# Group statistics of the last image taken 18 steps into layer 3, and its first loads issued from ScalarE's queue into other buffers

## Chip, core and metric

The kernel runs on one core of one Trainium2 chip. The metric is the time on the device in microseconds (us), from the first to the last instruction of that core and what lies around them. The median of three runs of the kernel before is 3160.31 us (3152.64 to 3162.91).

A core has five engines with a queue of their own each: TensorE (PE; its weight loads are listed apart as PEld), VectorE (DVE), ScalarE (ACT), GpSimd (POOL) and SyncE (SP). Each works off its queue in order and waits for semaphores. SP computes nothing here: it issues DMA transfers. ScalarE can issue them too.

## The reference

Four residual layers on four images of 256 channels and 48 x 48 points, each after a group norm without weights:

```
x = x + L0(gn(x))     # attention over 49 dilated neighbours
x = x + L1(gn(x))     # 3x3 convolution of signs
x = x + L2(gn(x))     # 3x3 convolution, ternary weights, scale alpha
x = x + L3(gn(x))     # box-window linear attention, 8 heads

gn(v): m, s = mean and var over the 8 channels of a group and all points
       (v - m) / sqrt(s + 1e-5)

L3(x): q, k = sigmoid(Wq x), sigmoid(Wk x);  v = Wv x / |Wv x|
       for w in 1, 2, 4:                     # windows of 48, 24, 12 points
         attn = q . box_w(k v^T);  norm = q . box_w(k)
         out_w = attn / (norm + 1e-6)
       Wout [out_1, out_2, out_4] + bout
```

So layer 3 needs from each image two numbers for every channel, the mean and one over the deviation of its group, taken over the whole of layer 2's output.

## The kernel before

**Two parts.** The first part computes layers 0 to 2 image by image, with other work laid into its gaps, and stores each image's result to `x3_d` in HBM. The second part, from about 1413 us on, is layer 3 for all images. For image 0, queries, keys and values are projected in the first part already, beside layers 0 to 2 of the last image (`project_first`); for each other image they are projected inside layer 3, one image ahead of their use.

**Order.** `InOrder` wraps every engine, so that the instructions of an engine run in the order of the program text. Plain `nc.scalar` calls, as the loads of `wout_sb` and `bout_sb`, are not wrapped, but stand in ScalarE's text ahead of everything of layer 3. The first SP transfer after pools are opened may move ahead of SP transfers of the text before it; the queries' first load does (1405.23 us, before the last store of x).

**The statistics** (class `Stats`). `take` adds one block's moments on VectorE. `end` makes the group values: two aggregations; a tiny matmul with `gmat` that averages over a group; four VectorE operations; a second tiny matmul; one addition; then `rsqrt`, which takes a root on ScalarE and refines it by five VectorE operations. Between these it calls `wait`, which lays in filler work. `layer2` ends with `stats.end` and writes the image's factors to `st3`, which only the projections of that image read. For the last image that is deep in layer 3.

**Layer 2's end.** `give` adds a convolution's output, times `alpha`, to x on VectorE. After the last third of the rows it stores x (`x3_d`), 384 KB.

**Layer 3's loop.** Its unit is a block: image `b`, half of the heads `ct`, and eight rows `rb`. A block has some ten steps. In step `n` TensorE makes the scores of step `n` (`s`, out of queries `qs` and keys `ks`), VectorE, ScalarE and GpSimd mask them into `sm`, and TensorE sums step `n - 2` (`acc`, out of `sm` and values `vs`). `ps_s` has two buffers and a step uses both, so scores wait for the masks of the step before. At the fifth step of a block (`WHOLE`) the window states are added; they are made of the keys and values of the row blocks that are seen whole (`state`, `window_state`).

Beside this, `advance` is called once in a step and lets every waiting job (a Python generator: projections, running sums of keys `k_sums`, norms, states) go one piece further. A job says by `yield n` for how many steps it wants to rest. `bank` gives the one spare PSUM bank to one job in a step. `until` calls `advance` again and again until something is made; these forced steps count as steps. `FETCH` is 3, the rest after a load is issued.

**First loads.** Ahead of the loop come the first block's queries (`load_q`) and the keys and values of `seen_first` = 4 row blocks (`load_kv`), all on SP: 192 KB each. SP's later loads in the text are those of `k_sums` into `kp` (192 KB each) and of the projections into `xr` (384 KB each).

**Memory.** Pools are laid one behind the other in the order of the text, and layer 3's pools begin where those of the first part began. A tile of layer 3 waits for all uses of the earlier tiles whose place it takes. By the order and the sizes in bytes of a partition, counted from there: the first part has `wts` (0 to 1792, `alpha` last in it), then x in four buffers of 9216 (the last image in the third and fourth, up to 38656), then two operands of the convolutions of 25600 (the last image's in the second, 64256 to 89856), then weights. Layer 3 has `wts3` (0 to 15104, `wout_sb` with 6144 first in it), `kvp` (keys 15104 to 33536, values to 51968), then queries, and `sm` from 126464. So the first four keys lay on the x of the third image and, with a corner, of the last; the first values lay on the x of the last image and the first operand.

Of the kernel before, what the change touches and what calls it, by code (L numbers as in the profile page):

```python
# [12 lines left out]
F32 = mybir.dt.float32  # L13
# [9 lines left out]
P = 128  # L23
B, C, H, W = 4, 256, 48, 48
HW = H * W
NCT = C // P

RB = 8
NRB = H // RB
NB = RB * W  # L30
# [45 lines left out]
HEADS, D = 8, 32  # L76
WINDOWS = (1, 2, 4)
NW = len(WINDOWS)
HALVES = [H // w // 2 for w in WINDOWS]
# [4 lines left out]
LAG = 2  # L84
# [75 lines left out]


SEED = float(0x5F3759DF)


def penalties():
# [103 lines left out]
def conv_preact_kernel(  # L269
# [105 lines left out]
    def start(job, ahead=False):  # L375
        active.insert(0 if ahead else len(active), [step + 1, job])
# [60 lines left out]
    def paced(jobs, pace):  # L437

        for job in jobs:
            start(job)  # L440
            yield pace
# [172 lines left out]
    with (  # L614
# [50 lines left out]
        class Stats:  # L665
# [6 lines left out]
                dve.bn_stats(self.st[:, ct, s, :], xt[ct][:, s * RB : (s + 1) * RB, :])  # L672

            def end(self, wait):
                mv = small.tile([P, NCT, 2], F32, tag="gn_mv", name="gn_mv")
                for ct in range(NCT):
                    dve.bn_aggr(mv[:, ct, :], self.st[:, ct])
                m = small.tile([P, NCT], F32, tag="gn_m", name="gn_m")
                v = small.tile([P, NCT], F32, tag="gn_v", name="gn_v")
                r = small.tile([P, NCT], F32, tag="gn_r", name="gn_r")  # L680
                wait(1.5)
                ps = ps_st.tile([P, NCT], F32, tag="st", name="gn_ps")
                pe.matmul(ps, gmat, mv[:, :, 0], start=True, stop=True)
                dve.tensor_copy(m, ps)

                dve.tensor_sub(v, mv[:, :, 0], m)
                dve.tensor_mul(v, v, v)
                dve.tensor_add(v, v, mv[:, :, 1])
                wait(2.5)
                ps = ps_st.tile([P, NCT], F32, tag="st", name="gn_ps")  # L690
                pe.matmul(ps, gmat, v, start=True, stop=True)
                dve.tensor_scalar_add(v, ps, GN_EPS)
                rsqrt(r, v, NCT)
                return m, r
# [686 lines left out]
        def layer2(b, stats):  # L1381
# [100 lines left out]
                fetch_x(b + 2, 0)  # L1482
            fill(2)
            late()
            fill(1.5)
            m3, r3 = stats.end(fill)
            dve.scalar_tensor_tensor(st3[:, b, 0, :], m3, -1.0, r3, ALU.mult, ALU.mult)
            dve.tensor_copy(st3[:, b, 1, :], r3)

# [100 lines left out]
        with (  # L1590
            tc.tile_pool(name="xtp", bufs=3) as xtp,
            tc.tile_pool(name="bandp", bufs=1) as bandp,
            tc.tile_pool(name="smx", bufs=2) as smx,
        ):

            spread = smx.tile([QB, NPH * K0, HP], F32, tag="spread", name="spread", bufs=1)
            pool.memset(spread, 0.0)
            load_constants()
            prelude(1)
            batch_norm()  # L1600
            side = itertools.chain(prepare_layer1(), prepare_layer2())
            first = ExitStack()

            def project_first():

                scr, ps = (
                    first.enter_context(tc.tile_pool(name=name, bufs=2, side="right", **kwargs))
                    for name, kwargs in (("scr0", {}), ("ps_0", {"space": PSUM}))
                )
                for name, src in (("q", wq), ("k", wk), ("v", wv)):  # L1610
                    proj[name] = wts3.tile([P, NCT, C], F32, tag=f"w{name}", name=f"w{name}_sb")
                    sync.dma_start(out=proj[name], in_=src.rearrange("(ct p) o -> p ct o", p=P))
                groups = [(a, ("k0", "v", "q0")) for a in range(NRB)]
                groups += [(a, ("k1", "q1")) for a in range(NRB)]
                proj["first"] = Projection(0, scr, ps, "ps", [P, 512]), groups
                start(paced(proj["first"][0].groups(groups), 1))
                while active:
                    advance()
                    yield 1.2

            for b in range(B):
                if b + 1 < B:
                    filler = conv0(b + 1, {})
                else:
                    ending.close()
                    wts3 = ctx.enter_context(tc.tile_pool(name="wts_qkv", bufs=1, side="right"))
                    filler = project_first()
                    masks = wts3.tile([P, NMASK], BF16, name="masks")
                    nc.gpsimd.dma_start(out=masks, in_=masks_in[:, 0:NMASK])
                stats = attend(b)  # L1630
                for _ in side:
                    fill(1.5)
                load_wl1(0)
                load_wl1(1)
                load_wl2(0)
                layer2(b, layer1(b, stats))
                if b + 2 < B:
                    prelude(b + 2)
                else:
                    fill_all()  # L1640
            first.close()


    with (
        tc.tile_pool(name="wts3", bufs=1, reuse_waits="tile") as wts,
        tc.tile_pool(name="kvp", bufs=2 * NRB, reuse_waits="tile") as kvp,
        tc.tile_pool(name="qp", bufs=2, reuse_waits="tile") as qp,
        tc.tile_pool(name="scr", bufs=2, reuse_waits="tile") as scr,
        tc.tile_pool(name="smp", bufs=LAG + 1, reuse_waits="tile") as smp,
        tc.tile_pool(name="op", bufs=2, reuse_waits="tile") as op,  # L1650
        tc.tile_pool(name="ps_s", bufs=2, space=PSUM, reuse_waits="tile") as ps_s,
        tc.tile_pool(name="ps_acc", bufs=1, space=PSUM, reuse_waits="tile") as ps_acc,
# [202 lines left out]
        def load_kv(b, ct, a):  # L1855

            chans, cols = slice(ct * P, (ct + 1) * P), slice(a * NB, (a + 1) * NB)
            ks = kvp.tile([P, NKC, P], F32, tag="ks", name="ks")
            sync.dma_start(out=ks.rearrange("p k n -> p (k n)"), in_=k_d[b][chans, cols])
            vs = kvp.tile([P, NKC, HG, D], F32, tag="vs", name="vs")  # L1860
            sync.dma_start(
                out=vs, in_=v_d[b][:, a * NKC : (a + 1) * NKC, ct * HG : (ct + 1) * HG, :]
            )
            kvs[b, ct, a] = ks, vs
            if (b, ct) not in states:
                states[b, ct] = scr.tile([P, NRB, NKC, D], F32, tag="state", name="state")
            start(state(b, ct, a), ahead=True)

        def state(b, ct, a):

# [36 lines left out]
            wides[i] = t  # L1907
            made.add(("window", i))

        def load_q(b, ct, rb):  # L1910
            qs = qp.tile([P, W, RB], F32, tag="qs", name="qs")
            sync.dma_start(
                out=qs.rearrange("p w r -> p (w r)"),
                in_=q_d[b][ct * P : (ct + 1) * P, rb * NB : (rb + 1) * NB],
            )
            return qs
# [319 lines left out]
        def finish(i, stage):  # L2236
# [66 lines left out]
        seen_first = HALVES[0] // RB + 1  # L2303
# [27 lines left out]
        def midway(i):  # L2331

            b, ct, rb = order[i]
            if (b, ct) == (0, 0) and 0 < rb <= NRB - seen_first:
                a = seen_first - 1 + rb
                until(("k", 0, 0, a), ("v", 0, a))
                load_kv(0, 0, a)
            if ct == NCT - 1:
                start(prepare(i))
            if i + 1 < len(order):  # L2340
                start(window_state(i + 1), ahead=True)
                nb, nct, nrb = order[i + 1]
                until(("q", nb, nct, nrb))
                qs[i + 1] = load_q(*order[i + 1])

        def done(i):

            b, ct, rb = order[i]
            finishing.append((i, blocks.pop(i).stage))
            nb, nct = b + (ct + 1) // NCT, (ct + 1) % NCT  # L2350
            if nb < B:
                for a in LOADS.get(rb, ()):
                    until(("k", nb, nct, a), ("v", nb, a))
                    load_kv(nb, nct, a)


        stream = [
# [102 lines left out]
```

## Time and profile before

| | us |
|---|---|
| median of three runs | 3160.31 |
| the profiled execution | 3175.78 |
| its span, first to last instruction | 3174.0 |
| TensorE busy in the span | 2852.3 |
| TensorE's mean granted clock | 0.952 of full |
| last convolution's end to first scores | 1412.88 to 1416.64 |
| queries issued, first keys issued, first values issued | 1405.23, 1413.92, 1416.15 |
| `wout_sb` issued, first `kp`, first `xr` issued | 1416.87, 1424.68, 1425.73 |
| ScalarE's first mask of layer 3 | 1418.01 |
| TensorE busy in 1410 to 1430, 1430 to 1450, 1450 to 1470 | 12.62, 15.76, 20.00 of 20 each |

All times within the program are from the span's start, in the profiled execution. A line of the timeline gives the start, the length, the engine, the operation with the tile it writes and those it reads, and in brackets how long the engine had been idle before and what it waited for. `SPq` and `ACTq` are transfers being issued by SP and ScalarE; the length is that of the issuing, not of the transfer. The wrapper has one line of code for all engines, so operations are told apart by their tiles and not by lines.

### The profile page before, as it was taken

How to read it: one execution, taken by the hardware profiler on the slowest of the kernel's cores; microseconds unless marked ns; L12 is line 12 of the kernel's file. 1: busy time of each engine (PE TensorE's matmuls, PEld its weight loads, DVE VectorE, ACT ScalarE, POOL GpSimd, SP SyncE). 2: the span in 40 equal slices, each digit the busy share in tenths (PEclk: the TensorE clock that was granted, in tenths of full speed). 3: DMA queues.
4: the chain of work that ended last, by engine and by line, in shares of the span. 5: the costliest groups of instructions: out<-in, count | busy, mean ns of one | idle time of the engine just before them, and what ended most of it. 6: DMA issues, size and time to landing. Idle time of an engine off the chain costs nothing.

```text
span 3174.0 us, 99454 instructions
## 1 busy us (share of the span) xinstructions
PE 2852.3 (90%) x43082; PEld 2034.6 (64%) x43082; DVE 1989.3 (63%) x3779; ACT 991.4 (31%) x1959; POOL 1368.6 (43%) x1963
## 2 busy tenths in 40 slices
PE   3678999899989987889998899998999999999999
PEld 2556868677767866576665456665656666567665
DVE  7976658747864842276777565776546775555454
ACT  0002211121011134326643235552336533333322
POOL 0000012002000313046788876787856787744443
PEclk9889799999999998889999899999999999999999
DMA  8756412441333145324555665655644455611322
GB/s 277 214 161 188 154 68 103 127 127 49 132 114 113 57 124 158 113 80 138 160 181 174 184 203 157 183 174 161 169 127 145 142 173 156 166 41 43 97 73 66
DMA packets 380040, 434.10 MB, mean 137 GB/s; under 512 B 129843, under 2 KB 335443, under 8 KB 378451
## 3 DMA queue, kind: packets, MB, share of 16 engines
q1 hardware_dynamic: 378403, 425.76, 43.4%
q8 instruction: 341, 5.59, 0.7%
q0 software_dynamic: 144, 1.17, 0.2%
q10 hardware_dynamic: 1056, 0.79, 0.1%
q14 instruction: 96, 0.79, 0.1%
HBM read 288.11 MB, written 140.68 MB: 135 GB/s over the span
## 4 chain that ended last, share of the span: by engine, by line
PE 63%; DVE 11%; ACT 3%; POOL 3%; DMA 3%; issue 3%; SPq 1%; ACTq 0%; DVEq 0%; POOLq 0%
PE s L265 17%; PE cv L265 15%; PE acc L265 15%; PE out_ps L265 6%; PE proj_ps L265 5%; PE ap L265 3%; DVE sm L265 2%; DVE l2v L265 2%; ACT sm L265 1%; DVE v L265 1%; POOL sm L265 1%; PE keys_ps L265 1%; SPq L265 1%; DVE x L265 1%; DVE k L265 1%
## 5 line engine op out<-in xcount | busy, mean ns | idle before, releaser
L265 DVE TENSOR_TENSOR sm<-s,masks 128x448 f32<-128x448 f32 (+9 forms) x1408 | 620.1, 496 | 451.2 <-PE s L265 392.4
L265 POOL TENSOR_TENSOR sm<-sm,masks 128x704 f32<-128x704 f32 (+11 forms) x512 | 596.5, 1186 | 495.8 <-DVE sm L265 495.2
L265 ACT ACTIVATE sm<-s 128x384 f32<-128x384 f32 (+2 forms) x736 | 440.8, 608 | 734.2 <-PE s L265 583.9
L265 PE MATMUL cv<-vx,wt 128*128 128x288 f32 x2080 | 566.7, 429 | 90.5 <-DVE vx L265 49.2
L265 PE MATMUL s<-qs,ks 32*128 32x320 f32 (+10 forms) x8704 | 593.5, 361 | 36.7 <-ACT sm L265 26.3
L265 PE MATMUL acc<-sm,vs 128*32 128x128 f32 (+19 forms) x18432 | 606.6, 276 | 2.5 <-issue 2.1
L265 PEld LDWEIGHTS s<-qs,ks 32*128 32x128 f32 x8704 | 397.8, 186 | 264.1 <-issue 124.3
L265 PEld LDWEIGHTS acc<-sm,vs 128*32 128x32 f32 x18432 | 443.1, 110 | 176.5 <-issue 124.5
L265 PEld LDWEIGHTS cv<-vx,wt 128*128 128x128 f32 x2080 | 406.9, 200 | 213.6 <-issue 53.3
L265 POOL MEMSET v<- 128x16 f32 (+1 forms) x120 | 18.6, 214 | 765.2 <-DVE vx L265 639.0
L265 PE MATMUL cv<-v,wl 128*128 128x384 f32 x1152 | 227.2, 358 | 25.8 <-DVE x L265 8.2
L265 PEld LDWEIGHTS cv<-v,wl 128*128 128x128 f32 x1152 | 217.1, 198 | 37.0 <-issue 16.9
L265 DVE TENSOR_SCALAR sm<-s 128x896 f32<-128x896 f32 (+1 forms) x96 | 110.8, 1154 | 112.0 <-PE s L265 93.6
L265 PE MATMUL s<-masks 24*128 24x192 bf16 (+3 forms) x1664 | 169.2, 284 | 0.8 <-issue 0.8
L265 POOL TENSOR_TENSOR v<-l2v,v 128x384 fp32r<-128x384 f32 x96 | 108.4, 1158 | 119.5 <-ACT v L265 110.7
L265 PE MATMUL cv<-pad,wl 128*128 128x384 bf16 x864 | 145.6, 331 | 5.1 <-ACT pad L265 5.1
L265 POOL TENSOR_TENSOR nhi<-nhi,nq 128x384 f32<-128x384 f32 x144 | 147.3, 1044 | 0.0
L265 PE MATMUL out_ps<-o,wout_sb 128*32 128x384 f32 x1152 | 121.3, 490 | 7.2 <-ACT ns L265 3.7
L265 PEld LDWEIGHTS <-wl 128*128 128x128 bf16 x864 | 84.5, 98 | 65.6 <-issue 8.1
L265 PE MATMUL out_ps<-stage,wout_sb 128*32 128x384 f32 x1152 | 121.3, 487 | 0.0
L265 PE MATMUL ap<-seen,xT 120*128 120x120 f32 (+3 forms) x832 | 120.8, 306 | 0.0
L265 DVE TENSOR_TENSOR pt<-cs 128x184 f32<-128x184 f32 x144 | 120.4, 840 | 0.1
(176 smaller groups left out, 3398.6 us busy)
## 6 DMA issues: line engine op xcount, KB each, us to landing
wt<-wt SPq DMA_DIRECT2D x48, 768.0 KB
kb_d<-pt SPq DMA_DIRECT2D x48, 576.0 KB
rc<-r_d SPq DMA_DIRECT2D x192, 144.0 KB
nhi<-kb_d SPq DMA_DIRECT2D x120, 192.0 KB
nlo<-kb_d SPq DMA_DIRECT2D x88, 192.0 KB
o_d<-stage SPq DMA_DIRECT2D x24, 576.0 KB
o<-o_d SPq DMA_DIRECT2D x24, 576.0 KB
wl<-wl_d SPq DMA_DIRECT2D x16, 768.0 KB
```

Source lines behind the costliest of these rows:

```text
L265: return lambda *args, **kwargs: self.tc.keep_in_program_order(op(*args, **kwargs))
```

## The change

It has four pieces.

- `Stats.end` becomes a generator, `ending(room)`, that yields where it waited and takes its PSUM tile from `room`. `end` drives it, so that all other statistics stay as they were.
- For the last image `layer2` returns its `stats` with the aggregation not begun. A new job `moments`, started ahead of the loop of layer 3, rests for `6 * FETCH` = 18 steps, then runs `ending` with the spare bank `ps_m`, waits for its turn at the bank each time, and writes `st3` through `keep_moments`.
- The first queries, keys and values are issued by ScalarE (`queue=act`), after `wout_sb` and `bout_sb`; the four keys first, then the four values.
- The pools change order: queries and `sm` come right after `wts3`; `kvp` has buffers only for the row blocks below `SEEN_FIRST` = 4, and a new `kvp2` has those for the other two. By the same count, queries lie at 15104 to 18176, `sm` to 58880, the first keys at 58880 to 71168 and the first values from there to 83456.

```diff
+SEEN_FIRST = HALVES[0] // RB + 1
...
             def end(self, wait):
+                todo = self.ending(lambda: ps_st.tile([P, NCT], F32, tag="st", name="gn_ps"))
+                while True:
+                    try:
+                        wait(next(todo))
+                    except StopIteration as done:
+                        return done.value
+
+            def ending(self, room):
...
-                wait(1.5)
-                ps = ps_st.tile([P, NCT], F32, tag="st", name="gn_ps")
+                yield 1.5
+                ps = room()
...
-                wait(2.5)
-                ps = ps_st.tile([P, NCT], F32, tag="st", name="gn_ps")
+                yield 2.5
+                ps = room()
...
             late()
+            if b == B - 1:
+                return stats
             fill(1.5)
-            m3, r3 = stats.end(fill)
+            keep_moments(b, *stats.end(fill))
+
+        def keep_moments(b, m3, r3):
+
             dve.scalar_tensor_tensor(st3[:, b, 0, :], m3, -1.0, r3, ALU.mult, ALU.mult)
             dve.tensor_copy(st3[:, b, 1, :], r3)
...
-                layer2(b, layer1(b, stats))
+                last_stats = layer2(b, layer1(b, stats))
...
-        tc.tile_pool(name="kvp", bufs=2 * NRB, reuse_waits="tile") as kvp,
         tc.tile_pool(name="qp", bufs=2, reuse_waits="tile") as qp,
+        tc.tile_pool(name="smp", bufs=LAG + 1, reuse_waits="tile") as smp,
+        tc.tile_pool(name="kvp", bufs=2 * SEEN_FIRST, reuse_waits="tile") as kvp,
+        tc.tile_pool(name="kvp2", bufs=2 * (NRB - SEEN_FIRST), reuse_waits="tile") as kvp2,
         tc.tile_pool(name="scr", bufs=2, reuse_waits="tile") as scr,
-        tc.tile_pool(name="smp", bufs=LAG + 1, reuse_waits="tile") as smp,
...
+        def load_kvs(b, ct, rows, queue=sync):
+
+            new = {}
+            for a in rows:
+                chans, cols = slice(ct * P, (ct + 1) * P), slice(a * NB, (a + 1) * NB)
+                new[a] = (kvp if a < SEEN_FIRST else kvp2).tile([P, NKC, P], F32, tag="ks", name="ks")
+                queue.dma_start(out=new[a].rearrange("p k n -> p (k n)"), in_=k_d[b][chans, cols])
+            for a, ks in new.items():
+                vs = (kvp if a < SEEN_FIRST else kvp2).tile([P, NKC, HG, D], F32, tag="vs", name="vs")
+                queue.dma_start(
+                    out=vs, in_=v_d[b][:, a * NKC : (a + 1) * NKC, ct * HG : (ct + 1) * HG, :]
+                )
+                kvs[b, ct, a] = ks, vs
+                if (b, ct) not in states:
+                    states[b, ct] = scr.tile([P, NRB, NKC, D], F32, tag="state", name="state")
+                start(state(b, ct, a), ahead=True)
...
+        def moments():
+
+            yield 6 * FETCH
+            todo = last_stats.ending(lambda: ps_m.tile([P, 512], F32, tag="st", name="gn_ps")[:, 0:NCT])
+            while True:
+                try:
+                    next(todo)
+                except StopIteration as done:
+                    keep_moments(B - 1, *done.value)
+                    return
+                yield from bank(1, 0.0)
...
+        start(moments())
         for mo in range(NCT):
             start(k_sums(mo))
...
-        qs = {0: load_q(*order[0])}
-        for a in range(seen_first):
-            load_kv(0, 0, a)
+        qs = {0: load_q(*order[0], queue=act)}
+        load_kvs(0, 0, range(seen_first), queue=act)
```

More of the change, by code (lines that the diff above doesn't have):

```diff
@@ L1853, in inverse @@
             made.add(("norm", b, rb))
[L1855 to L1867, printed above, removed]
+        def load_kvs(b, ct, rows, queue=sync):
[13 more added lines that the diff above has]
+                start(state(b, ct, a), ahead=True)
         def state(b, ct, a):
@@ L1908, in window_state, with load_q @@
             made.add(("window", i))
-        def load_q(b, ct, rb):
+        def load_q(b, ct, rb, queue=sync):
             qs = qp.tile([P, W, RB], F32, tag="qs", name="qs")
-            sync.dma_start(
+            queue.dma_start(
                 out=qs.rearrange("p w r -> p (w r)"),
@@ L2301, in conv_preact_kernel @@
         start(in_turn(norms(b, rb) for b in range(B) for rb in range(NRB)))
-        seen_first = HALVES[0] // RB + 1
+        seen_first = SEEN_FIRST
         until(("q", 0, 0, 0), *((what, 0, *at) for a in range(seen_first) for what, at in (("k", (0, a)), ("v", (a,)))))
-        qs = {0: load_q(*order[0])}
-        for a in range(seen_first):
-            load_kv(0, 0, a)
+        qs = {0: load_q(*order[0], queue=act)}
+        load_kvs(0, 0, range(seen_first), queue=act)
         LOADS = {2: (0,), 3: (1, 2), 4: (3, 4), 5: (5,)}
@@ L2336, in midway @@
                 until(("k", 0, 0, a), ("v", 0, a))
-                load_kv(0, 0, a)
+                load_kvs(0, 0, (a,))
             if ct == NCT - 1:
@@ L2353, in done @@
                     until(("k", nb, nct, a), ("v", nb, a))
-                    load_kv(nb, nct, a)
+                    load_kvs(nb, nct, (a,))
         stream = [
```

## The prediction

> **What bounds the kernel now.** I read first the page's shares and its slices, to see which engine is full in which stage.
>
> ```profile
> span 3174.0 us, 99454 instructions
> PE 2852.3 (90%) x43082; PEld 2034.6 (64%) x43082; DVE 1989.3 (63%) x3779; ACT 991.4 (31%) x1959; POOL 1368.6 (43%) x1963
> ...
> PE   3678999899989987889998899998999999999999
> ...
> PEclk9889799999999998889999899999999999999999
> ```
>
> One slice is 79.4 us. TensorE is the bound nearly everywhere, so time that it stands idle at the edited place reaches the end. That place is the passage from layer 2 to layer 3, at 1413 us. I read next the chain of waits there (start, length, what), then the timeline (in brackets the idle time before an instruction and what ended it).
>
> ```profile
> 1395.14 17.74 PE cv L265 x96
> ...
> 1412.91 0.63 DVE x L265
> ...
> 1413.55 2.53 DMA x_d<-x
> ...
> 1417.57 7.26 DMA ks<-k_d
> 1424.83 0.14 issue
> 1424.97 2.51 PE s L265 x36
> ```
>
> ```profile
> 1415.02 0.30 PEld L265 LDWEIGHTS gn_ps<-gn_mv,gmat 128*128 128x128 f32 x2 [2.48 <-DVE gn_mv L265]
> ...
> 1416.24 0.30 PEld L265 LDWEIGHTS gn_ps<-gn_v,gmat 128*128 128x128 f32 x2 [0.92 <-DVE gn_v L265]
> ...
> 1416.64 1.15 PE L265 MATMUL s<-qs,ks 32*128 32x320 f32 x16
> ...
> 1416.86 0.20 ACT L265 ACTIVATE rsq_s<-gn_v 128x2 f32<-128x2 f32 x1 [18.22 <-DVE gn_v L265]
> 1416.87 0.43 ACTq L1656 DMA_DIRECT2D wout_sb<-in_wout_dram  x1
> ...
> 1419.26 1.58 SPq L265 DMA_DIRECT2D vs<-v_d  x1
> ```
>
> The reader is to see three things. The last convolution ends at 1412.88 and the first scores start at 1416.64: 3.76 us, in which TensorE does only the statistics. ScalarE's queue stands still for 18.22 us before `rsq_s`, and the load of `wout_sb` leaves 0.01 us after it. And the chain does not run through the statistics at all: it runs through the store of x and the third load of keys, which lands at 1424.83. The clock, in a table of one-microsecond windows (last three columns: granted clock, DMA share, GB/s), completes it:
>
> ```profile
> 1417.00:1418.00 1.00, 0.87 (x20) 0.48 (x12) 0.77 (x5) 0.06 (x1) 0.00 (x0) 1.00 0.53 157
> 1418.00:1419.00 1.00, 0.00 (x0) 0.00 (x0) 0.96 (x5) 0.49 (x1) 0.00 (x0) 0.52 1.02 282
> ...
> 1423.00:1424.00 1.00, 0.00 (x0) 0.00 (x0) 1.00 (x3) 0.55 (x2) 0.10 (x1) 0.50 1.09 359
> ...
> 1429.00:1430.00 1.00, 1.00 (x32) 0.86 (x28) 0.00 (x0) 0.08 (x1) 0.00 (x0) 1.00 0.73 216
> ```
>
> From 1418 to 1424.7 the DMA engines are full, and the clock is halved until about 1428.5.
>
> **What the Trainium skill says.** "DMA: Bandwidth & Descriptors", section "Queues, rings and completion order": each issuing queue has its own ring on each of the same 16 engines, a ring is consumed in its order, and an engine takes turns between rings packet by packet. The trace agrees: the keys issued at 1417.57, beside the output weights on the other ring, took 7.26 us, against 2.53 us for a store of twice the size. "TensorE: Matmul & The Clock Gate", section "Part 1: The HAM clock gate": after an idle window of about 3.4 us the clock is halved, and it comes back after about as long a busy one. Here 3.76 us of near idleness precede 0.50, and it returns some 3.5 us after work becomes dense at 1424.97. "ScalarE: Activation LUTs", section "What ACT_TABLE_LOAD costs": 1283 ns, and about 1380 ns of draining; the trace has 1283 ns for each of its 21, and doesn't show the draining.
>
> **Part 1, the statistics leave the passage.** Two pairs of tiny matmuls, two aggregations and some twelve VectorE operations of 0.15 to 0.3 us go. Taken alone this saves less than 3.76 us: the first keys were issued only at 1413.92, behind the store of x in SP's order, and the store and these keys (589 KB) were moving until 1416.2 (windows of 261, 270 and 58 GB/s). So the keys would have held the scores until about 1416.3 anyway; the saving without the load edit is about 0.3 us. It also frees ScalarE's queue from the wait for `rsq_s`.
>
> **Part 2, the loads move.** They are nine: one of queries, four of keys, four of values, 192 KB each. In ScalarE's order they stand behind `wout_sb` and `bout_sb`, which are written ahead of them. When can `wout_sb` leave? ScalarE's layer 2 work ends with a table load at 1398.64, so the queue is free. But by the sizes in the code `wout_sb` (6144 bytes in a partition) is the first tile of layer 3 and lies where the pool `wts` was, and that pool ends with `alpha`, which the last `give` reads until 1413.53. I take it that `wout_sb` waits for this read. Before, `rsq_s` hid that wait. So: `wout_sb` at 1413.57, 0.43 to issue; `bout_sb` 0.55; queries at about 1414.65, first keys 1415.1. The queries were issued at 1405.23 before, so this is later by 9.4 us, and the first keys by 1.2.
>
> What is worse, 768 KB of `wout_sb` are now ahead of queries and keys in the same ring. On SP nothing holds back the two `kp` loads (192 KB each, before at 1424.68, behind the last values) and `xr` (384 KB, before at 1425.73): I expect them right behind the store, at 1413.9 to 1415. Until the first keys land these must move: store 393 KB, `kp` 393, `xr` 393, `wout_sb` 786, queries 197, keys 197, together 2359 KB. The windows from 1417.5 to 1424.8 moved about 2160 KB in 7.2 us, so 0.30 MB in a microsecond: 7.9 us from 1414.2, so 1422. If the ring of `wout_sb` gets more than half I get 1421; if `kp` and `xr` come later, 1571 KB, so 1419.5. I take 1421.5: the first scores 4.9 us later than before.
>
> From there the pace is set by the masks, two score buffers being all there are: second scores about 4.2 us later (half clock), third again 4.2, so 1429.9 against 1424.97, also +4.9. Before, the third waited about 1.0 us for its keys (ScalarE was done at 1423.95), and now their keys are there in time; but the first scores now run at half clock (2.2 us for 1.15), which takes it back. The new places of the tiles are otherwise harmless: `sm` now overlaps the last image, whose store lands at 1416.08, before the first mask; the fourth keys and the values overlap layer 2's last operand, free at 1412.88. What follows until 1446, when TensorE waits for the windows' states, is a chain of the same steps and shifts as a whole. Sum of parts 1 and 2: +4.9, between +1.5 and +7.
>
> **Part 3, the statistics inside layer 3.** Eighteen steps counted with the forced ones come out near 1475 to 1490. In 1470 to 1490 TensorE is busy 19.53 of 20, VectorE 15.91, ScalarE 12.06. First half: two aggregations (0.25 each), four operations of 0.16, with gaps 1.2 us on VectorE, beside TensorE's accumulation. Second half: one operation, then a table load of 1.28 and the root of 0.20 on ScalarE, for which VectorE waits, then seven operations (1.3). Behind VectorE's wait stand the next step's masks, and behind those the scores. About 2.9 us against some 0.8 us of slack in a step of 3.4 leaves up to 2. Then the sigmoids' table comes back (1.28); before, one such load stood at 1445.63, where ScalarE was idle for 4.45 us after it, and the root's at 1397.36 in idle time too. The trace before shows no such switch in the steady part: at least 0 (all of it beside slack), at most 4 (both loads with the page's draining, an estimate). I take +2. The two uses of the bank push projections of image 1 back by two steps, far from due: 0.
>
> The split pools keep as many buffers per row block as before, and keys before values is without effect later, where single blocks are loaded: 0.
>
> **Sum.** +4.9 + 2 = +7 in the profiled execution: its own time was 3175.78 (span 3174.0), so about 3183. The median of the runs, 3160.31, lies 15.5 lower; carried over to it: 3167. That is +0.2%. A measurement of this kernel can tell about 0.3% (9.5 us) from no change.
>
> **Rivals.**
> *A, the loads leave early.* If `wout_sb` need not wait for `alpha`, all loads go out from 1398.6 and are there at 1412.88. Scores start 3.7 us earlier, the third ones 1.0 more, and the gap is too short for the half clock, worth about 3 (6.7 us of matmuls in 1418 to 1428 at half rate); less 2 of part 3: -6, 3154; at best -10. For it: the 18 us of idle ScalarE queue. Against: the overlap of addresses.
>
> *B, slower: ScalarE is held by issuing.* Eleven issues now stand ahead of its first mask. With full rings an issue took SP 1.58 us (values at 1419.26, queries at 1426.63), and a load of `kp`, due next, left SP only at 1424.68, so completions can hold issues back. Nine at 1.58 from 1414.65 end at 1428.9 instead of the 1423.8 when scores want a mask: +5 on top, +12, so 3172. It decides from a mean issue of 1.0 us. For it: full DMA; against: a mean issue of 0.45 for the rest, and keys need few descriptors.
>
> *C, a ripple.* From 1730 to 1775 TensorE is busy only 25.6 of 45 and GpSimd 39.25: image 0's norms are late there. Two shifted steps could move that by 8 us, either way: with +7, 3175 or 3159.
>
> **Chances.** Forecast 0.42 (0.34 within 0.3%, 0.08 slower), A 0.20 (0.12 faster, 0.08 within), B 0.28 (0.22 slower, 0.06 within), C 0.10 (0.06 slower, 0.03 faster, 0.01 within). Together: faster 0.15, within 0.49, slower 0.36. The range from 3150 to 3181 takes in A's middle, B, and the unknown costs of parts 2 and 3.
>
> **What would show it.** Right: `wout_sb` issued at 1413.6, scores at about 1421, no `gn_ps` before them, two table loads near 1480. Wrong: queries issued before 1413 (A); ScalarE still issuing values while finished scores wait (B); or scores before 1417 with `wout_sb` ahead of them, which would mean the rings share otherwise than I assumed.

## The result, and the profile after

The changed kernel takes 3205.60 us in the median of five runs (3194.39 to 3209.57); the kernel before took 3160.31 beside it. The ratio is 1.0131, with a 95% interval from 1.0111 to 1.0151: 1.3% slower, 45 us. The forecast was 3167, with a range up to 3181.

The page of the changed kernel, its shares and then its slices (here 80.1 us each):

```profile
span 3203.2 us, 99462 instructions
...
PE 2852.2 (89%) x43082; PEld 2031.6 (63%) x43082; DVE 2000.6 (62%) x3779; ACT 994.1 (31%) x1968; POOL 1369.6 (43%) x1963
...
PE   3678999898989977879997999898999999999999
...
PEclk9789799999999987889998999899999999999999
```

TensorE is as long busy as before (2852.3 us there). The loss is time in which it stands. Three slices from the passage on are one tenth lower than the same slices were before, and one, the 23rd, is one tenth higher. The lower ones are the 18th (1361 to 1441, the passage), the 22nd (1682 to 1762) and the 26th (2002 to 2082).

**What to compare.** The first part of the program is the same in both kernels, but it ended at 1402.8 in this profiled execution and at 1412.9 in that of before; over the sixteen kernels profiled here it ended between 1395.2 and 1412.9. So I compare times from the end of the last convolution. From there to the last instruction it is 1761.1 us before and 1800.4 after: +39.3. Kernels whose medians equal that of before lie between -4.8 and +4.0 by this measure, so a single such number is good to about 5 us.

The score products (8704 matmuls `s<-qs,ks`) come in the same order in every kernel, so the start of the n-th of them, from the last convolution's end, tells where a kernel falls behind. Differences to the kernel before, in us, worked out from the traces; image 0 ends at 2176, the first half of image 1 at 3264:

| n-th score product | 0 | 200 | 350 | 1400 | 1850 | 2300 | 3200 | 4400 | end |
|---|---|---|---|---|---|---|---|---|---|
| changed kernel | 4.7 | 6.0 | 7.9 | 4.6 | 11.0 | 9.5 | 35.2 | 44.3 | 39.3 |
| e1, two turns only | 0.0 | 0.4 | -0.9 | -4.4 | 2.5 | 1.3 | 28.2 | 34.3 | 30.5 |
| e12, one turn | 4.7 | 6.8 | 10.2 | 10.5 | 11.9 | 12.4 | 11.3 | 12.6 | 10.1 |
| e11, passage mended | -3.1 | -0.2 | -0.2 | 0.4 | 5.4 | 4.7 | 6.6 | 10.2 | 6.4 |

The passage costs about 6 us, near what was foreseen. The rest arises far behind the change, most of it in the first half of image 1. Between the 1400th and the 1850th product the changed kernel is up to 54 us behind for a while and has nearly caught up at the 1700th (13.6): the same steps of work come there in another order, as is shown below.

**The passage.** The chain of waits of the changed kernel there:

```profile
1385.07 17.72 PE cv L266 x96
...
1402.81 0.63 DVE x L266
...
1404.34 7.97 DMA kp<-kf_d
...
1412.33 0.33 ACTq L266
...
1412.70 0.45 ACTq L266
...
1414.87 0.88 ACT sm L266 x2
...
1415.80 2.86 PE s L266 x16
```

Its timeline (start, length, engine, operation, idle time before it and what ended that):

```profile
1403.46 0.44 ACTq L1671 DMA_DIRECT2D wout_sb<-in_wout_dram  x1
1403.87 1.16 SPq L266 DMA_DIRECT2D kp<-kf_d  x2
...
1405.23 7.43 ACTq L266 DMA_DIRECT2D ks<-k_d  x4
...
1411.21 2.09 PE L266 MATMUL s<-qs,ks 32*128 32x320 f32 x16 [8.44 <-DMA ks<-k_d]
```

`wout_sb` leaves 0.69 us after the last convolution, right after the last `give`; first scores come 8.44 us after it, 3.76 before. ScalarE issues keys and values until its first mask at 1414.87, 1.4 us after VectorE's first (1413.48): it is held, but little. By the chain one of its issues, that of the fourth keys at 1412.33, was held until `kp`, which SP had issued, had landed (1404.34 and 7.97 later).

**Where the larger part sits.** The same 160 us, counted from the start of the span, in the stretch table (busy time and number of instructions for PE, PEld, DVE, ACT, POOL, then granted clock, DMA share, GB/s). Before:

```profile
1950.00:2110.00 160.00, 154.27 (x3557) 101.89 (x3552) 114.79 (x207) 91.15 (x192) 127.32 (x193) 0.98 0.52 160
```

and after, followed by the waits of TensorE in 1930 to 2110 (what waited, for what, us in total, times, longest):

```profile
1950.00:2110.00 160.00, 140.22 (x3038) 90.97 (x3034) 102.91 (x181) 80.23 (x168) 117.06 (x156) 0.91 0.50 155
```

```profile
PE proj_ps L266 <- ACT sg L266: 18.0, 3, 7.7
PE s L266 <- ACT sm L266: 1.5, 1, 1.5
```

Before, the longest of these waits was another, and short:

```profile
PE proj_ps L265 <- ACT sq L265: 4.2, 1, 4.2
```

Every engine does less, the clock falls from 0.98 to 0.91, and TensorE makes 3038 matmuls in place of 3557. It stands three times for some 6 us because a projection's sigmoid (`sg`) is not done. ScalarE's own line at one of these places, and SP's queue ahead of it:

```profile
1955.34 0.49 ACT L266 ACTIVATE sg<-proj_ps 128x384 f32<-128x384 f32 x1 [8.28 <-DMA q_d<-sg]
```

```profile
1940.79 0.34 SPq L266 DMA_DIRECT2D nr<-n_d  x1
1941.23 0.38 SPq L266 DMA_DIRECT2D nq<-qr_d  x1
...
1949.26 1.53 SPq L266 DMA_DIRECT2D nlo<-kb_d  x1
1950.89 0.38 SPq L266 DMA_DIRECT2D qr_d<-kt  x1
1951.31 0.43 SPq L266 DMA_DIRECT2D q_d<-sg  x1
```

The sigmoid wants one of two `sg` buffers, whose store (`q_d<-sg`) stands in SP's order behind 16 loads for a block's norms (1941.2 to 1950.8; the expectations of e7, e9 and e13 give 30 and 14). Nothing of this touches the statistics or the first loads. An earlier trace of it is in the output products, `out_ps`, of the first finished block (block 6). Before:

```profile
1673.29 0.83 PE L265 MATMUL out_ps<-o,wout_sb 128*32 128x384 f32 x8
```

After:

```profile
1704.92 1.51 PE L266 MATMUL out_ps<-o,wout_sb 128*32 128x384 f32 x8 [2.38 <-ACT ns L266]
```

It comes 31.6 us later (41.7 from the last convolution), and its result is stored at 1750.86 in place of 1693.21. That gave the theory.

**The theory, "order".** Running the program's own order of jobs step by step shows that the spare bank is given away or held in every step from 70 to 137. The statistics take steps 85 and 88. All projections of image 1 behind them move on: the last value product of row block 4 goes from step 124 to 130, that of row block 5 from 139 to 141.

The bank is not what then delays block 6: it stands free from step 142 to 149, and block 6's output product does not ask for it. It waits for its preparation (`prepare`), three multiplications by one over the norms on GpSimd (`o<-o,rc`). GpSimd's time is shared out among the jobs like the bank, by `pool_turn`, and the jobs are asked in the order of a list, in which that of row block 4's values stands ahead of the preparation. After its last value product a row block scales its values on GpSimd. Before, row block 4 did this in steps 126 to 136, and block 6's preparation got all three of its turns in step 137. Now the scaling fills steps 136 to 138; the preparation gets one turn in step 139, and running sums and norms take the next ones. The other two come in step 150, where the loop forces steps because it needs block 6 done. GpSimd's trace shows the three multiplications together before:

```profile
1658.14 2.92 POOL L265 TENSOR_TENSOR o<-o,rc 128x384 f32<-128x384 f32 x3
```

and after one alone, the other two 45 us later, with a product of TensorE waiting for them:

```profile
1666.74 1.01 POOL L266 TENSOR_TENSOR o<-o,rc 128x384 f32<-128x384 f32 x1
...
1711.63 1.95 POOL L266 TENSOR_TENSOR o<-o,rc 128x384 f32<-128x384 f32 x2
1712.68 1.51 PE L266 MATMUL out_ps<-o,wout_sb 128*32 128x384 f32 x8 [4.97 <-POOL o L266]
```

So block 6's output product moves from step 141 to 153. The loop has to force nine steps for block 6 at its position 78, where it forced eleven for block 7 at position 89. From there on norms, stores and projections fall on other steps than in the kernel before, and the total stays at about the same number of steps (570 before, 569 now). The rival is that the moved work costs by itself: the statistics' instructions, the late loads, the new buffers.

### The profile page after: what moved, and what is told of

It is laid out like the page before. It is cut to its first block, busy times and chain, and to the rows that moved or that the text cites. A ratio compares the mean times of both kernels' runs of the same rounds, so it can differ in the third digit from the quotient of the medians.

```text
span 3203.2 us, 99462 instructions
## 1 busy us (share of the span) xinstructions
PE 2852.2 (89%) x43082; PEld 2031.6 (63%) x43082; DVE 2000.6 (62%) x3779; ACT 994.1 (31%) x1968; POOL 1369.6 (43%) x1963
## 4 chain that ended last, share of the span: by engine, by line
PE 61%; DVE 13%; POOL 4%; ACT 3%; DMA 3%; issue 2%; SPq 1%; ACTq 0%; DVEq 0%; POOLq 0%
PE s L266 17%; PE cv L266 15%; PE acc L266 14%; PE out_ps L266 5%; PE proj_ps L266 5%; DVE sm L266 3%; PE ap L266 3%; DVE l2v L266 2%; POOL sm L266 2%; SPq L266 1%; ACT sm L266 1%; DVE v L266 1%; POOL nhi L266 1%; PE keys_ps L266 1%; DVE x L266 1%
## 5 line engine op out<-in xcount | busy, mean ns | idle before, releaser
L266 PE MATMUL s<-qs,ks 32*128 32x320 f32 (+10 forms) x8704 | 602.4, 363 | 48.2 <-ACT sm L266 29.5
```

The source lines that it names most:

```text
L266: return lambda *args, **kwargs: self.tc.keep_in_program_order(op(*args, **kwargs))
```

## The experiments

Medians are of the runs of each kernel; ratios are against the kernel before on the same chip (its medians: 3165.04 for e1 to e4, 3163.74 for e5 to e8, 3163.40 for e9 to e11, 3168.35 for e12 to e14). The last column is the difference from the last convolution to the end, in one profile.

| kernel | median us | ratio, 95% interval | layer 3, us |
|---|---|---|---|
| changed kernel | 3205.60 | 1.0131 [1.0111, 1.0151] | +39.3 |
| e1 two turns only | 3194.54 | 1.0093 [1.0074, 1.0111] | +30.5 |
| e2 statistics late | 3180.48 | 1.0057 [1.0040, 1.0074] | +9.5 |
| e3 loads on SP | 3197.44 | 1.0103 [1.0084, 1.0121] | +37.6 |
| e4 late, weights last | 3177.87 | 1.0043 [1.0027, 1.0058] | +8.7 |
| e5 one turn only | 3163.52 | 0.9997 [0.9986, 1.0009] | -1.5 |
| e6 six turns only | 3172.20 | 1.0023 [1.0012, 1.0035] | +8.4 |
| e7 changed, one store on ScalarE | 3205.79 | 1.0131 [1.0108, 1.0153] | +35.2 |
| e8 before, the same | 3165.06 | 1.0000 [0.9984, 1.0017] | -4.8 |
| e9 changed, stores a step earlier | 3209.01 | 1.0147 [1.0112, 1.0182] | +39.3 |
| e10 before, the same | 3174.00 | 1.0027 [1.0014, 1.0040] | +10.3 |
| e11 passage mended, statistics hidden | 3170.99 | 1.0022 [1.0009, 1.0034] | +6.4 |
| e12 changed, one turn | 3177.85 | 1.0026 [1.0014, 1.0039] | +10.1 |
| e13 changed, norm loads split | 3203.56 | 1.0116 [1.0096, 1.0136] | +37.5 |
| e14 before, the same | 3169.32 | 1.0001 [0.9984, 1.0018] | +4.0 |

**e1: the two turns alone, in the kernel before.** The job issues no instruction; only the order of the others changes. By the program it is exactly that of the changed kernel, step by step.

```diff
+        def two_turns():
+
+            yield 6 * FETCH
+            yield from bank(1, 0.0)
+            yield from bank(1, 0.0)
...
+        start(two_turns())
         for mo in range(NCT):
             start(k_sums(mo))
```

> The kernel before, with one job added that does nothing but claim the spare bank for one step twice, from the 18th step on (it gets steps 85 and 88); statistics, loads and pools stay as before. Theory 'order' (two turns taken from the fully booked bank re-order the projections, norms and stores of images 0 and 1, and that is what costs): most of the +45 us, so +33 to +42 us over the kernel before, 3193 to 3202 us, with the same gaps of TensorE between 1950 and 2225 us. Rival 'instructions' (the loss is in the moved statistics' own instructions and in the later first loads): nothing is issued here, so within 5 us of the kernel before.

Measured: +29.5 us in the median, +30.5 in layer 3, a little less than "order" gave. Its stretch and its waits, for the same window as above:

```profile
1950.00:2110.00 160.00, 139.65 (x3002) 90.26 (x3006) 102.67 (x181) 81.19 (x169) 118.51 (x159) 0.92 0.51 157
```

```profile
PE proj_ps L265 <- ACT sg L265: 18.6, 3, 7.8
```

They are nearly those of the changed kernel, without one instruction of statistics and with all loads where they were. The rival falls for the larger part of the loss.

**e2: the statistics where the bank is free.**

```diff
         def moments():
 
-            yield 6 * FETCH
+            yield 27 * FETCH
```

> The changed kernel with the statistics 81 steps into layer 3 in place of 18, where the bank is booked by nobody (steps 148 and 149): all side jobs then run in the steps of the kernel before. Theory 'order': only the passage (+5.0 us in the profile) and up to 4 us of the statistics are left, so +3 to +9 us over the kernel before, 3163 to 3169 us. Rival 'instructions', or any loss by the new pools and queues: it stays near the changed kernel, +35 us or more.

Measured: +9.5 in layer 3 and +15.4 in the median, so some 30 us of the loss are gone; by the median it is 6 us more than the upper end of what I expected. It loses 6.0 in the passage and 4.6 at the statistics, of which about 1.5 come back.

**e3: the loads back on SP**, in the new buffers.

```diff
-        qs = {0: load_q(*order[0], queue=act)}
-        load_kvs(0, 0, range(seen_first), queue=act)
+        qs = {0: load_q(*order[0])}
+        load_kvs(0, 0, range(seen_first))
```

> The changed kernel with its first queries, keys and values issued by SP again, in the new buffers; the statistics stay 18 steps into layer 3. Theory 'order': only the passage gets its 5 us back, last convolution to first scores 3.4 to 4 us, so 3 to 8 us below the changed kernel, +36 to +42 us over the kernel before. Rival 'queue' (the loads through ScalarE delay everything that follows): back to within 10 us of the kernel before.

Measured: +32.4 in the median and +37.6 in layer 3, which is only 1.7 below the changed kernel. Layer 3 alone is within what was expected, and not by the stated path: the first scores were still 8.1 us after the last convolution, not 3.4 to 4. ScalarE issued `wout_sb` at 1407.42, before SP's first keys at 1408.26, and these were then waited for. So the queue of the loads hardly matters (1.5 us at the 200th product). That 768 KB of weights leave ahead of the keys is what is left; e4 tests it.

**e4: weights behind queries, keys and values, with the statistics late.**

```diff
-        nc.scalar.dma_start(out=wout_sb, in_=wout.rearrange("(kt p) o -> p kt o", p=P))
-        nc.scalar.dma_start(out=bout_sb, in_=bout.rearrange("(ct p) -> p ct", p=P))
...
         load_kvs(0, 0, range(seen_first), queue=act)
+        act.dma_start(out=wout_sb, in_=wout.rearrange("(kt p) o -> p kt o", p=P))
+        act.dma_start(out=bout_sb, in_=bout.rearrange("(ct p) -> p ct", p=P))
```

> The changed kernel with the statistics 81 steps in, as in e2, and the output weights and their bias issued by ScalarE after the first queries, keys and values instead of ahead of them. Theory 'order' with my account of the passage: queries and the first keys no longer wait behind 768 KB, first scores at most 3.5 us after the last convolution, so -5 to +1 us against the kernel before, and 4 to 9 us below e2. Rival (ScalarE is held by the issuing itself, not by the weights): as e2, within 2 us.

Measured: +12.8 in the median, 2.6 below e2: a miss, and the rival was nearer. The timeline of e4:

```profile
1405.72 1.15 PE L266 MATMUL s<-qs,ks 32*128 32x320 f32 x16 [0.71 <-DVE x L266]
...
1409.40 2.44 ACTq L266 DMA_DIRECT2D vs<-v_d  x4
...
1412.43 1.91 ACTq L266 DMA_DIRECT2D bout_sb<-in_bout_dram  x1
1414.44 0.87 ACT L266 ACTIVATE sm<-s 128x384 f32<-128x384 f32 x2 [24.96 <-DMA qs<-q_d]
```

First scores now start 0.71 us after the last convolution. But their mask waits behind ScalarE's issues until 1414.44, and TensorE waits 8.42 us for it. Of the 7.7 us won at the first scores 2.6 are left at the 200th product. This is the prediction's rival B, at a place where it decides.

**e5 and e6: one turn, six turns**, again in the kernel before. The edit of e1 for one turn; for six there are four such lines more than in e1.

```diff
             yield 6 * FETCH
-            yield from bank(1, 0.0)
             yield from bank(1, 0.0)
```

> As e1, but the added job takes one turn at the bank (step 85) and no second. Theory 'order' in its sharp form (the loss comes when the last value projections of image 1 are pushed onto step 141, where block 6's output product takes the bank before): with one turn less that product keeps its step, and norms and forced steps fall as in the kernel before, so within 5 us of it. Rival (every turn taken from a full bank costs alike): half of e1, +12 to +17 us.

> As e1, but with six turns at the bank (steps 85 and 88 to 92). By the order of the jobs six lost steps put norms and forced steps back to those of the kernel before. Theory 'order' in its sharp form: within 6 us of the kernel before, although three times as many turns are lost as in e1. Rival (turns cost alike): three times e1, +60 us or more; and if projections simply get too late, at least e1's +30.

Measured: one turn -0.2 us (0.9997), six turns +8.5 (1.0023; the expectation had 6). So the cost is not so much for a turn: none for one, 30 for two, 8 for six. What matters is who is pushed in front of whom. By the program's order, one turn leaves block 6's preparation its turns on GpSimd in steps 137 to 139, and the output product comes in step 142. Six turns push the values of row block 4 so far back that they come after the preparation, which has its turns in step 137 as before, and the product keeps step 141. In both, the forced steps stay where they were. In the trace of e6 the first output product starts at 1664.92 (259.0 from the last convolution; 260.4 before, 302.2 after). The sharp form in e5's expectation had the right result for another reason: it took step 141 of the bank for the place of the loss, but with two turns the bank is free in the eight steps after it.

**e12: the changed kernel with one turn.** All instructions, loads and buffers of the change stay; both products of the statistics are made in step 85.

```diff
+            yield from bank(1, 0.0)
             while True:
                 try:
                     next(todo)
                 except StopIteration as done:
                     keep_moments(B - 1, *done.value)
                     return
-                yield from bank(1, 0.0)
```

> The changed kernel with a single edit: the job of the statistics claims the bank once, at step 85, and makes both of its products in that one turn, in place of steps 85 and 88. Same instructions, same loads, same place. Theory 'order': one turn leaves norms and forced steps as in the kernel before (e5), so only passage (6 us) and the statistics' own time (2 to 5 us) are left: +8 to +14 us over the kernel before, some 30 us below the changed kernel. Rival (the second product so close behind the first stalls TensorE, or the loss hangs on what else the change does): +25 us or more.

Measured: +9.5 in the median, +10.1 in layer 3, so about 30 us below the changed kernel. Its stretch and TensorE's waits, as above:

```profile
1950.00:2110.00 160.00, 153.74 (x3606) 102.71 (x3606) 114.00 (x206) 91.79 (x192) 126.09 (x192) 0.99 0.52 159
```

```profile
PE proj_ps L266 <- ACT sq L266: 4.3, 1, 4.3
```

The waits for `sg` are gone and the clock is back. GpSimd's three multiplications for block 6 start at 1662.27, 1668.30 and 1672.26, within 11 us. With e1 this settles the cause: the second turn at the bank, and nothing that the change issues, makes 30 of the 39 us.

**e7, e9, e13: why the new order is worse.** Three edits of the changed kernel try to take away the waits for `sg`, each with a control in the kernel before (e8, e10, e14). None moves a job to another step. e7 and e8:

```diff
-            sync.dma_start(out=second[b][chans, cols], in_=t)
+            (act if b > 0 else sync).dma_start(out=second[b][chans, cols], in_=t)
```

> The changed kernel, with one of the two stores of a projection (the one that frees the sigmoid's buffer) issued by ScalarE in place of SP, for images 1 to 3. Theory: in the first half of image 1 sigmoids wait 26.3 us for stores that stand in SP's order behind the 30 loads of a block's norms, and TensorE's next projection waits 18.0 us for them; with the store on another queue this goes: 12 to 20 us below the changed kernel, still +20 to +33 us over the kernel before. Rival (TensorE's wait is replaced by GpSimd's lateness at the norms, or the issuing slows ScalarE's masks): within 6 us of the changed kernel.

> The same edit in the kernel before, as a control: there sigmoids wait only 1.9 us for such stores, so no gain is to be had by it; -4 to +6 us, the upper end if the issuing on ScalarE delays masks.

e9 and e10:

```diff
-            yield 1
             first, second = (qr_d, q_d) if name == "q" else (k_d, kf_d)
+            if b == 0:
+                yield 1
             sync.dma_start(out=first[b][chans, cols], in_=kt)
             sync.dma_start(out=second[b][chans, cols], in_=t)
+            if b > 0:
+                yield 1
```

> The changed kernel, with both stores of a projection (images 1 to 3) issued in the step of its sigmoid, ahead of the next step's jobs; all jobs keep their steps. Theory 'store behind the burst': the buffers of sigmoid and copy come free before the norms' 30 loads are issued, TensorE's 18.0 us of waiting for sigmoids in image 1 mostly go, 10 to 18 us below the changed kernel. Rival (the same turns of the bank are late wherever the stores stand, and norms' own loads wait instead, so GpSimd and TensorE are late there): within 5 us of the changed kernel.

> The same edit in the kernel before, as a control: little waiting for stores to take away (1.9 us for sigmoids, 6.6 us for values), so -5 to +4 us.

e13 and e14:

```diff
-            loaded = [load(ct) for ct in range(NCT)]
-            yield FETCH
+            loaded = [load(0)]
+            yield 2
+            loaded.append(load(1))
+            yield FETCH - 2
```

> The changed kernel with the loads of a block's norms issued in two halves two steps apart (the wait for them is shortened by as much, so every job keeps its steps). In image 1 the 14 loads in a row hold SP for 9.6 us (1941.2 to 1950.8) while two projections' stores stand behind them. Theory 'burst': TensorE's 18.0 us of waiting for sigmoids go down to 10 or less and 8 to 15 us are won against the changed kernel. Rival (TensorE's loss in image 1 isn't held by the burst alone, or the norms get their second half too late): within 5 us of the changed kernel, or above it.

> The same edit in the kernel before, as a control: nothing waits there for stores behind the norms' loads for more than 1.9 us; -3 to +6 us, the upper end if the second half comes late for GpSimd.

Measured: 1.0131, 1.0147 and 1.0116 against 1.0131 of the changed kernel: no gain, none, and at most 5 us. Each time TensorE's waits for `sg` shrink (9.8, 13.7 and 12.1 us in place of 18.0 in layer 3), and other waits grow. In e7 one sees how; ScalarE's part of the timeline:

```profile
1946.32 0.33 ACTq L266 DMA_DIRECT2D q_d<-sg  x1
...
1953.76 0.33 ACTq L266 DMA_DIRECT2D kf_d<-sg  x1
1954.19 0.49 ACT L266 ACTIVATE sg<-proj_ps 128x384 f32<-128x384 f32 x1 [4.60 <-DMA nhi<-kb_d]
1958.49 0.51 ACT L266 COPY kt<-sg 128x384 f32<-128x384 f32 x1 [3.81 <-DMA qr_d<-kt]
```

The store is issued early (1946.32; its sister `qr_d<-kt`, left on SP, at 1954.11), but ScalarE's next issue is held until 1953.76, by the trace until a load of the norms has landed, and then the copy `kt` waits for the other store, still behind the norms on SP. Among the controls e10 costs 10.6 us (1.0027) although it changes no job's step. That was not foreseen; I did not trace it. So that projections meet the norms' loads is what the traces show at these places, but no edit has shown that it holds the 25 us of image 1. More buffers for `sg` were not tried: one takes 1.5 KB of a partition, and 0.25 KB are free. That the second turn costs these 25 us is shown; through which wait it does so stays open.

**e11: all that was learned, put together.** Statistics in steps 160 and 161, where TensorE waits anyway; ScalarE issues queries and keys alone; values and then weights on SP (ScalarE's loads of the weights go, as in e4).

```diff
-            yield 6 * FETCH
+            yield 31 * FETCH
...
-                queue.dma_start(
+                sync.dma_start(
                     out=vs,
...
         load_kvs(0, 0, range(seen_first), queue=act)
+        sync.dma_start(out=wout_sb, in_=wout.rearrange("(kt p) o -> p kt o", p=P))
+        sync.dma_start(out=bout_sb, in_=bout.rearrange("(ct p) -> p ct", p=P))
```

> The changed kernel with three places mended: statistics 93 steps into layer 3, in steps 160 and 161, where TensorE waits 7.77 us for GpSimd's norms anyway; values on SP; output weights and bias on SP after them, so that ScalarE issues only queries and keys. Theory: the order is the one of before, first scores some 0.7 us after the last convolution as in e4 and masks no longer behind issues, statistics hidden: -4 to 0 us against the kernel before. Rival (statistics cost 3 us wherever they stand in layer 3, values are late behind the store of x): +2 to +6 us.

Measured: +7.6 us (1.0022), so the rival was nearer. The passage is no worse than before (first scores 3.1 us earlier, but only 0.2 are left of it at the 200th product). The statistics cost 5 us at their place, and another 4 are lost in the second half of image 1. The timeline of VectorE and GpSimd in e11 shows why the place was not free:

```profile
1721.44 0.16 DVE L266 COPY gn_m<-gn_ps 128x2 f32<-128x2 f32 x1 [0.48 <-PE gn_ps L266]
1721.60 2.52 POOL L266 TENSOR_TENSOR sm<-sm,masks 128x448 f32<-128x448 f32 x2
1721.63 1.04 DVE L266 TENSOR_TENSOR gn_v<-gn_mv,gn_m 128x2 f32<-128x2 f32 x1
1722.71 1.44 DVE L266 TENSOR_TENSOR gn_v<-gn_v 128x2 f32<-128x2 f32 x1
...
1730.59 0.92 DVE L266 TENSOR_SCALAR rsq_u<-rsq_u 128x2 f32<-128x2 f32 x1
```

Eight operations on two columns, 0.16 us nearly everywhere in e12, take 0.75 to 1.44 here, beside GpSimd's masks, norms and sums. The chain from 1720.48 to 1733.48, waits included, takes 13 us; in e12, at step 85, it took 4.3 (1474.67 to 1478.94). No version tried beats the kernel before.

## Why the prediction was wrong

- **Part 1, the statistics leave: not tested alone.** "About 0.3" was to be saved without the load edit, and no run moves the statistics and leaves all loads. e11 is 0.2 ahead at the 200th product, but its loads are other ones too.
- **Part 2, the loads: right in kind, in size with luck.** +4.9 was forecast, +4.7 measured at the first scores and +6.0 at the 200th. `wout_sb` left after `alpha`'s last read, at the foreseen 0.69 us after the convolution; `kp` and `xr` moved ahead beside it. But the sum has two errors that offset each other. The windows of the kernel before hold 2.02 MB in 7.2 us (281 GB/s), not 2.16, so its rate was too high; and from 1404 to 1411.2, where the scores start, 2.06 MB moved (286 GB/s), not 2.36. By its own figures `kp` and `xr` behind the keys should bring the keys 2 us forward; e3 has them there, and 0.4 came. What e4 and e11 confirm is that the weights ahead of the keys are the cost: without them the first scores start 0.71 us after the convolution. Rival A falls, as the weights did wait. Rival B's sign came: from 1404.55 to 1414.77 nine issues took 1.1 us each, and it was to decide from 1.0. But as the first scores were late too, it cost 1.4 us at ScalarE's first mask and not 5; in e4, where they are early, it takes most of what was won.
- **Part 3, the statistics' own time: right within its bounds.** +2, from 0 to 4, was forecast; the two table loads came at 1481.55 and 1486.85. The changed kernel loses 1.8 us more from the 200th to the 350th product, where e1 gains 1.3: 3.2 for the statistics. In e2 and e11, at other steps, they cost 4.6 and 5.
- **Part 3, the bank: here it failed.** The step was: "The two uses of the bank push projections of image 1 back by two steps, far from due: 0." They cost 30.5 us in e1. The projections were indeed far from due. But I looked only at when the pushed projections are due, not at whom they push in turn: the bank is given away in every step up to 137, so the shift lasted, and the pushed values then took GpSimd's turns in steps 136 to 138 ahead of block 6's preparation, which the loop does wait for.
- **Rival C: the kind right, the reach too short.** It named the late norms of image 0, where the changed kernel does lose (4.6 us behind at the 1400th product, 11.0 at the 1850th, 9.5 at the 2300th). It allowed 8 us either way, from the idle time of that one stretch, and left out that every later job falls on another step too. The 25 us in the first half of image 1 lie outside the stretch.

The parts add up: 6 in the passage, 3 for the statistics and 30.5 for the order make about 39.5, against 39.3 measured. That they meet so closely is luck, as one profile is good to about 5 us; that the medians lie 45 apart and not 39 is of that order too.

## What to carry to other kernels

Where jobs share a resource that is given away in every step, two turns for a tiny job are not priced by that job's time. Follow who is pushed, and what those pushed do afterwards on other shared engines, until free turns take up the shift, and see whether it lies past a point that the main loop waits for. Here the turns were taken at a PSUM bank, and the delay came through GpSimd. Such an order answers in jumps (0, 30 and 8 us for one, two and six turns), so test the shift alone, by a job that takes the turns and does nothing. Before a load is moved to another queue, ask what large transfer leaves ahead of it, and what is queued behind its issues.

## What was not expected of the hardware

- In e11 eight of VectorE's operations on 128x2 elements took 0.75 to 1.44 us while GpSimd worked on SBUF data; in e12 the same ones took 0.16 or 0.17, one 0.53. The Trainium skill, "SBUF — State Buffer", section "Terms", says that the two engines share a pair of ports, which is locked for a whole instruction, so that the other blocks. The trace agrees in kind: the operation of 1722.71 ends at 1724.15, as GpSimd's masks (1721.60 to 1724.12) end. Not every operation is held: a reciprocal at 1728.65 (0.17) and a copy at 1733.33 (0.15) ran beside GpSimd's work in the usual time.
- By the trace, an issue on ScalarE's queue was held until a transfer of another queue had landed: 4.60 us before the sigmoid in e7, for a load that SP had issued, and in the changed kernel's passage for `kp`. What a wait is put down to is inferred from the profile, and no run tests why it is there. In e7, moving a store off SP's queue thus did not free it from SP's loads.
